# Spectral mixing weights loaded once and copied to four partition bands by TensorE, in a Fourier tokenizer with a transformer block

## The chip, the cores and the metric

The kernel runs on one core of one Trainium2 chip. The metric is the device time of one execution in microseconds (us), as the median of several runs. A core has a matrix engine (TensorE, PE in the profile, with its weight loads shown as PEld), a vector engine (VectorE, DVE), a scalar engine (ScalarE, ACT), a general engine (GpSimd, POOL) and a queue engine (SyncE, SP). Any of the last three may issue DMA transfers. SBUF is the on-chip memory of 128 partitions, PSUM the memory that TensorE writes to.

## The reference, cut to what matters

A batch of 64 images of 256 x 256 is lifted to C = 32 channels and passed through four Fourier layers. In each, the spectrum's lowest modes (12 rows from the top and 12 from the bottom, by 12 columns) are multiplied by complex weights that mix the channels. The result joins 77 text tokens and goes through one attention and one feed-forward layer.

```python
h = jnp.concatenate([x, gx, gy], axis=-1)
v = jnp.transpose(h @ p_w + p_b, (0, 3, 1, 2))          # 64 x 32 x 256 x 256
for i in range(4):
    W1 = fw1[i, ..., 0] + 1j * fw1[i, ..., 1]            # 32 in x 32 out x 12 x 12
    W2 = fw2[i, ..., 0] + 1j * fw2[i, ..., 1]
    x_ft = jnp.fft.rfft2(v)
    out_ft[:, :, :12, :12] = einsum('bixy,ioxy->boxy', x_ft[:, :, :12, :12], W1)
    out_ft[:, :, -12:, :12] = einsum('bixy,ioxy->boxy', x_ft[:, :, -12:, :12], W2)
    x1 = jnp.fft.irfft2(out_ft)
    x2 = einsum('bcxy,cd->bdxy', v, w_w[i]) + w_b[i]
    v = batchnorm(x1 + x2)                               # relu, but after the last
out = einsum('bcxy,cu->bxyu', v, q_w) + q_b              # 64 x 256 x 256
h = concatenate([out, txt], axis=1)                      # 64 x 333 x 256
h = h + attention(layernorm(h))
h = h + ffn_on_the_top_half_of_tokens(layernorm(h))
```

The weights `fw1` and `fw2` of one layer are 1.18 MB each, in f32, with the input channel first.

## The kernel before

The program is a sequence of stages. `forward_first` (L215) transforms the input images into the first spectrum `xh`. Then, for each Fourier layer `i`, `mix` (L410) multiplies the spectrum by the weights and writes the result to DRAM (`mix_d`). Between two mixes `layer` (L526) goes through all 64 images: it transforms back, adds the 1 x 1 product, applies the normalisation and the relu, and transforms the new values forward, storing a piece of the next spectrum for each image (`xh<-xo`, L783). After the fourth mix the constants of the transformer are loaded (from L843), the first image rows are read (`am`, L944; `hp`, L964) and the transformer runs.

*How a mix is tiled.* The 12 columns of modes are cut in 3 groups `g` of 4. The four columns of a group stand on four bands of 32 partitions, with the 32 input channels of a column in each band. So `xh` and the weight tiles `wm0`, `wm1` (one for each of `fw1`, `fw2`) have 128 partitions. A row of `mix` (loop over `kp`, 12 of them) takes two rows of modes: 48 matmuls (L437) with one band of `xh` as the stationary operand and one band of `wm` as the moving one. ACT copies the PSUM result to `e` (L449). ACT and DVE build from it the two parts of the output block `ob` (L454 to L457) and the sums for the normalisation (L460 to L474). SP stores the block by two DMAs (L475). There are three `ob` buffers in turn, cleared once by POOL (L421). After the loop the DVE chain and the square root (L482 to L510) give the scale and shift of the layer.

*How the weights come in.* `mix_weights` (L375) gives a function `piece(m)` for eight pieces: two weight tensors by four blocks of 8 output channels. A piece is a tile `wn` of 128 partitions, into which the same block is loaded four times, once for each band (L387), each time shifted by one column so that an index of column 0 in band `k4` is the weight of column `k4`:

```python
wn[C * k4:C * k4 + C, 0:n - 2 * k4],
fw[i, :, 8 * oh:8 * oh + 8].rearrange("c o k l r -> c (o k l r)")[:, 2 * k4:],
```

Then four copies bring the real and imaginary parts into the slots of `wm`: ACT into slots 0 (negated, L402) and 1 (L404), DVE into slots 3 and 4 (L406). Slot 5 is cleared (L392) and slot 2 filled with the 1 x 1 weights (L393) by POOL, with the first piece of each tensor. All the copies read `wn` with a stride of 1152 bytes between neighbouring output channels.

*Order.* For `i` = 0 the loads go on SP's queue, two pieces after the image loop of `forward_first`, and two after each of the three groups of its last transform; `wn` has two buffers. For the later layers the loads are on POOL's queue with four buffers: four pieces, then the load of the first 56 images of the spectrum (`xh` early, L826), the last 8 on SP (`xh` late, L829), `squares` (L513, which ends with the copy of `u2`, L523), and four more pieces. The buffers of `wn`, `xh` and `wm` lie over those of the layer before, so that a load waits for its last reader there. Elsewhere the order is written out, but the mixing weights and the constants stand in the order that a scheduler gives. In the program before, the ACT queue issues most of the transformer's constants (L854 to L899) among the rows of the fourth mix.

Of the kernel before, what the change touches and what calls it, by code (L numbers as in the profile page):

```python
# [17 lines left out]
C = 32  # L18
M = 12
# [134 lines left out]
def tile_fno_fusion_transformer(ctx: ExitStack, tc: tile.TileContext, a, cst_d, grid_d, out):  # L154
# [57 lines left out]
    w4 = [w4all[:, i, :] for i in range(L)]  # L212
    w0row = const.tile([128, 4, C], F32, name="w0row")

    def forward_first(xh, weights):  # L215


        u2 = const.tile([128, C], F32, name="u2_0")
# [1 line left out]
        with tc.tile_pool(name="f0", bufs=1) as fp, tc.tile_pool(name="f0i", bufs=3) as ip, \  # L220
# [41 lines left out]
                        accum_out=sq[:, b0 // 2 + n:b0 // 2 + n + 1],  # L262
                    )

            weights(0)
            weights(1)

            pw, pb = a["L0_tok_p_w"], a["L0_tok_p_b"].rearrange("(o c) -> o c", o=1)
            pwR = fp.tile([128, C], F32, name="pwR")
# [45 lines left out]
                    n += 1  # L315
            nc.scalar.copy(xm, ps[:, 0, :kn * B])

            for kyg in range(3):
                for ri in range(2):
                    t2 = [pq.tile([128, 2, 512], F32, name="xps") for _ in range(2)]  # L320
                    for j in range(4):
                        nc.tensor.matmul(
                            t2[j // 2][:, j % 2, :kn * B],
                            lhsT=px[32 * j:32 * j + KX, kyg, ri].rearrange("p q c -> p (q c)"),
                            rhs=xm[32 * j:32 * j + KX], start=True, stop=True, skip_group_check=True,
                        )
                    for j in range(2):
                        k0 = 2 * kn * j
                        nc.vector.tensor_tensor(
                            xh[:, kyg, ri, k0:k0 + 2 * kn, :].rearrange("p (j k) b -> p j k b", j=2),  # L330
                            t2[j][:, :, :kn * B].rearrange("p j (k b) -> p j k b", b=B),
                            g[:, kyg, ri, k0:k0 + 2 * kn, :].rearrange("p (j k) o -> p j k o", j=2)
                            .to_broadcast([128, 2, kn, B]),
                            ALU.add,
                        )
                weights(2 * kyg + 2)
                weights(2 * kyg + 3)


            mo = fp.tile([128, 4], F32, name="mo")  # L340
# [34 lines left out]
    def mix_weights(i, wmp, wnp):  # L375

        wms = [wmp.tile([128, 3, M, 6, C], F32, name=f"wm{half}") for half in range(2)]

        def piece(m):
            half, oh = divmod(m, 4)
            wm, fw = wms[half], a[f"L0_tok_fw{half + 1}"]
            n = 8 * M * M * 2
            wn = wnp.tile([128, n], F32, name="wn")
            for k4 in range(4):
                (nc.gpsimd if i else nc.sync).dma_start(  # L387
                    wn[C * k4:C * k4 + C, 0:n - 2 * k4],
                    fw[i, :, 8 * oh:8 * oh + 8].rearrange("c o k l r -> c (o k l r)")[:, 2 * k4:],
                )  # L390
            if oh == 0:
                nc.gpsimd.memset(wm[:, :, :, 5, :], 0.0)  # L392
                nc.gpsimd.tensor_copy(  # L393
                    wm[:, :, :, 2, :].rearrange("p g k o -> p (g k) o"),
                    w4[i].rearrange("p (o c) -> p o c", o=1).to_broadcast([128, 3 * M, C]),
                )
            v = wn.rearrange("p (o k g q r) -> p g k o q r", o=8, k=M, g=3, q=4)
            for slot, ri in ((4, 1), (3, 0), (1, 0), (0, 1)):
                s_ = v[:, :, :, :, 0, ri]
                d_ = wm[:, :, :, slot, 8 * oh:8 * oh + 8]  # L400
                if slot == 0:
                    nc.scalar.mul(d_, s_, -1.0)  # L402
                elif slot == 1:
                    nc.scalar.copy(d_, s_)  # L404
                else:
                    nc.vector.tensor_copy(d_, s_)  # L406

        return wms, piece

    def mix(i, lhs, wm, u2):  # L410


        halves = [slice(0, 128)] if B == 64 else [slice(0, B), slice(64, 64 + B)]
# [2 lines left out]
        with tc.tile_pool(name="mo", bufs=1) as op, tc.tile_pool(name="me", bufs=3) as ep, \  # L416
# [8 lines left out]
            nc.vector.memset(fr, 0.0)  # L425
            fin = op.tile([128, 2, C], F32, name="fin")
            nc.vector.memset(fin, 0.0)
            for kp in range(M):
                ps = pp.tile([128, 4, 512], F32, name="mps")
                wk, k0 = wm[2 * kp // M], 2 * kp % M  # L430
                for g in range(3):
                    for ri in range(2):
                        w0 = 32 * ri
                        for kk in range(2):
                            for k4 in range(4):
                                band = slice(C * k4, C * k4 + C)
                                nc.tensor.matmul(  # L437
                                    ps[64 * kk:64 * kk + B, k4, 128 * g + w0:128 * g + 128],
                                    lhsT=lhs(band, g, ri, 2 * kp + kk),
                                    rhs=wk[band, g, k0 + kk, 2 - 2 * ri:6 - 3 * ri, :].rearrange("p s o -> p (s o)"),  # L440
                                    start=ri == 0, stop=ri == 1, skip_group_check=True,
                                )
                e = ep.tile([128, 3, 4, 4, C], F32, name="e")
                a_ = ep.tile([128, 12, 2, C], F32, name="a_")
                o0, o1 = (
                    ob[kp % NB][:, p, :, :KX].rearrange("p o (n k) -> p n k o", k=M) for p in range(2)
                )
                for hv in halves:
                    nc.scalar.copy(  # L449
                        e[hv].rearrange("p g q s o -> p q g (s o)"),  # L450
                        ps[hv, :, 0:384].rearrange("p q (g s) -> p q g s", g=3),
                    )
                    ev = e[hv].rearrange("p g q s o -> p (g q) s o")
                    nc.scalar.mul(o1[hv, 0], ev[:, :, 2, :], -1.0)  # L454
                    nc.scalar.copy(o1[hv, 1], ev[:, :, 1, :])
                    nc.vector.tensor_copy(o0[hv, 0], ev[:, :, 1, :])
                    nc.vector.tensor_copy(o0[hv, 1], ev[:, :, 2, :])  # L457
                    nc.vector.tensor_copy(f0[hv, kp], ev[:, 0, 1:3, :])
                    for n, (us, fs) in enumerate(((0, 1), (3, 2))):
                        nc.vector.scalar_tensor_tensor(  # L460
                            a_[hv, :, n, :], ev[:, :, us, :], 2.0, ev[:, :, fs, :], ALU.mult, ALU.add
                        )
                    if kp == 0:
                        nc.vector.tensor_mul(acc[hv], a_[hv], ev[:, :, 1:3, :])
                    else:
                        nc.vector.tensor_mul(a_[hv], a_[hv], ev[:, :, 1:3, :])
                        nc.vector.tensor_add(acc[hv], acc[hv], a_[hv])
                if kp == 0:
                    nc.vector.tensor_add(fin[0:B, 1, :], e[0:B, 0, 0, 1, :], e[0:B, 0, 0, 0, :])
                for kk in range(2):  # L470
                    to = (M - kp) % M if kk == 0 else M - 1 - kp
                    hv = slice(64 * kk, 64 * kk + B)
                    if kk or kp != M // 2:
                        nc.scalar.copy(fr[hv, to], e[hv, 0, 0, 1:3, :])  # L474
                    nc.sync.dma_start(  # L475
                        mix_d[i][:, :, 2 * kp + kk, :], ob[kp % NB][hv].rearrange("b p o k -> b p (o k)")
                    )
# [331 lines left out]
    st = None  # L809
    acc = None  # L810
    for i in range(L):
        with tc.tile_pool(name="wn", bufs=4 if i else 2, reuse_waits="tile") as wnp, \
                tc.tile_pool(name="xh", bufs=1, reuse_waits="tile") as xp, \
                tc.tile_pool(name="wm", bufs=1, reuse_waits="tile") as wmp:
            wm, piece = mix_weights(i, wmp, wnp)
            if i == 0:
                xh = xp.tile([128, 3, 2, KX, B], F32, name="xh")
                u2 = forward_first(xh, piece)
                lhs = lambda band, g, ri, k: xh[band, g, ri, k, :]
            else:  # L820
                xh = xp.tile([128, B, 3, 2, KX], F32, name="xh")
                early = max(B - 8, 0)
                for m in range(4):
                    piece(m)
                if early:
                    nc.gpsimd.dma_start(  # L826
                        xh[:, :early].rearrange("p b g r k -> p b (g r k)"), xh_d[i - 1][:, :early]
                    )
                nc.sync.dma_start(  # L829
                    xh[:, early:].rearrange("p b g r k -> p b (g r k)"), xh_d[i - 1][:, early:]  # L830
                )
# [384 lines left out]
```

## Time and profile before

| what | value |
|---|---|
| time, median of 3 runs | 11381.7 us (11377.09 to 11388.17) |
| the profiled execution: its own time, its span | 11393.82 us, 11392.0 us |
| mean granted TensorE clock | 0.975 |
| busy: PE, DVE, ACT, POOL | 10594.2, 8460.5, 6496.0, 1477.9 us |
| first mix, from the first loads of weights to the last row | about 60 to 170 us |
| second, third and fourth mix, from `u2` to the end of the rows | 2554 to 2645, 5586 to 5685, 8633 to 8747 us |
| start of the transformer: load of the first `am` | 8763.1 us |

The profile is of one execution, and its times are microseconds from the start of the span. A line of the timeline gives the start, the length, the engine, the line of the kernel, the operation with output and input tile, and how many were merged ("x32"). In square brackets stands the idle time of the engine before it and what ended that. An engine with a "q" (SPq, ACTq, POOLq) is the queue that issues DMAs. A line of the waits gives who waited for whom: total time, number of waits, and the longest. The clock is a share of full speed, and the DMA share is how busy the 16 DMA engines of the core were.

### The profile page before, as it was taken

To read this page: it belongs to the slowest core of one execution; us is meant where nothing else is said; L and a number is where in the kernel's file an instruction comes from. 1 tells how busy PE (TensorE), PEld (TensorE's weight loads), DVE (VectorE), ACT (ScalarE), POOL (GpSimd) and SP (SyncE) were. 2 spreads that over 40 slices of the span, in tenths; PEclk is the share of its full clock that TensorE was granted. 3 is DMA by queue.
4 is the path that set the end of the run, shared out by engine and by line. 5 is a ranking of instruction groups with operands and counts; after the bars stand their busy time and mean duration, and the time that the engine had idled before them with its cause. 6 is when DMAs were issued, how large, how long until landed. Compare 5 with 4: busy or idle time off the path is not lost. (4 is left out here: it accounts for less than half of the span.)

```text
span 11392.0 us, 408517 instructions
## 1 busy us (share of the span) xinstructions
PE 10594.2 (93%) x182038; PEld 5729.6 (50%) x182038; DVE 8460.5 (74%) x10405; ACT 6496.0 (57%) x10697; POOL 1477.9 (13%) x2243
## 2 busy tenths in 40 slices
PE   6999999997999999999699999999995999999998
PEld 3555555543444444444344444444443666666666
DVE  5888888886777777777677777777775666666665
ACT  5777777775656655665556566565653333333333
POOL 0111111110000000000100000000001333333333
PEclk7999999998999999999899999999997999999999
DMA  7776676769999999999899999999998555555553
GB/s 233 248 248 244 247 250 246 248 238 326 378 383 376 383 379 375 376 380 380 296 374 383 379 383 380 377 373 371 382 376 279 224 222 224 228 230 227 229 227 135
DMA packets 977151, 3485.52 MB, mean 306 GB/s; under 512 B 151320, under 2 KB 200856, under 8 KB 905368
## 3 DMA queue, kind: packets, MB, share of 16 engines
q1 hardware_dynamic: 906880, 3376.23, 77.5%
q0 software_dynamic: 61360, 79.44, 3.1%
q8 instruction: 1424, 23.33, 0.8%
q10 hardware_dynamic: 7144, 3.72, 0.1%
q14 instruction: 343, 2.81, 0.1%
HBM read 1761.87 MB, written 1696.92 MB: 304 GB/s over the span
## 5 line engine op out<-in xcount | busy, mean ns | idle before, releaser
L721 ACT ACTIVATE ring<-ring 128x1024 f32<-128x1024 f32 x3072 | 3115.8, 1014 | 1182.0 <-PE ring L710 1116.4
L699 DVE STREAM_TRANSPOSE t<-vo 128x2048 f32<-128x2048 f32 x1536 | 3465.1, 2286 | 20.5 <-DVE vo L687 0.5
L710 PE MATMUL ring<-vo,w 32*32 32x512 f32 x49152 | 2411.8, 600 | 85.8 <-ACT vo L685 71.0
L687 DVE TENSOR_SCALAR vo<-ring 128x1024 f32<-128x1024 f32 x1280 | 1544.7, 1221 | 1195.4 <-PE ring L673 806.4
L685 ACT ACTIVATE vo<-ring 128x1024 f32<-128x1024 f32 x1792 | 1792.0, 1023 | 1043.3 <-PE ring L673 494.5
L732 PE MATMUL ring<-t,cst 32*32 32x512 f32 x49152 | 2072.6, 599 | 47.1 <-issue 40.8
L732 PEld LDWEIGHTS ring<-t,cst 32*32 32x32 f32 x49152 | 911.6, 103 | 924.9 <-issue 617.6
L710 PEld LDWEIGHTS ring<-vo,w 32*32 32x32 f32 x49152 | 802.2, 103 | 1071.6 <-issue 398.9
L611 POOL TENSOR_TENSOR ams<-ams,bns 48x512 f32<-48x512 f32 x384 | 401.4, 1045 | 6980.6 <-DMA ams<-mix 6710.2
L662 PE MATMUL ring<-cst,y 24*128 24x256 f32 x16384 | 1228.0, 402 | 76.2 <-DVE vo L687 58.2
L673 PE MATMUL ring<-vin,ws 32*32 32x512 f32 x32768 | 1281.2, 602 | 18.6 <-issue 13.2
L662 PEld LDWEIGHTS ring<-cst,y 24*128 24x128 f32 x16384 | 787.6, 185 | 989.7 <-DVE vo L687 389.0
L650 DVE STREAM_TRANSPOSE y<-ring 128x1024 f32<-128x1024 f32 x384 | 762.9, 1987 | 327.1 <-PE ring L642 326.2
L662 PE MATMUL ring<-mv,y 29*128 29x256 f32 x8192 | 703.8, 404 | 36.6 <-ACT ring L721 19.7
L662 PEld LDWEIGHTS ring<-mv,y 29*128 29x128 f32 x8192 | 455.2, 185 | 368.8 <-ACT ring L721 211.3
L766 PEld LDWEIGHTS ring<-cst,zt 128*128 128x128 f32 x4608 | 533.2, 193 | 178.3 <-ACT vo L685 114.3
L742 ACT COPY half<-ring 128x1024 f32<-128x1024 f32 x192 | 194.4, 1013 | 727.2 <-PE ring L732 727.1
L1165 POOL DMA_DIRECT2D out_dram<-o x1024 | 510.9, 507 | 660.6 <-DVE o L1160 617.6
L721 ACT ACTIVATION_READ_ACCUMULATOR ring<-ring 128x1 f32 x3072 | 584.9, 190 | 0.0
L766 PE MATMUL ring<-cst,zt 128*128 128x96 f32 x4608 | 565.3, 279 | 7.9 <-DVE zt L750 7.3
L750 DVE STREAM_TRANSPOSE zt<-ring 128x1024 f32<-128x1024 f32 x192 | 377.0, 1963 | 244.6 <-PE ring L732 244.6
L642 PE MATMUL ring<-ams,cst 49*128 49x512 f32 (+1 forms) x1536 | 450.3, 642 | 104.9 <-POOL ams L611 38.4
(367 smaller groups left out, 9812.4 us busy)
## 6 DMA issues: line engine op xcount, KB each, us to landing
v<-vo SPq DMA_DIRECT2D x3072, 512.0 KB, 7.9
vin<-v SPq DMA_DIRECT2D x2048, 512.0 KB, 9.1
ch<-v SPq DMA_DIRECT2D x512, 1024.0 KB, 12.6
mix<-ob SPq DMA_DIRECT2D x96, 512.0 KB, 5.7
ams<-mix SPq DMA_DIRECT2D x384, 96.0 KB, 8.0
xin<-in_x_dram SPq DMA_DIRECT2D x16, 1024.0 KB, 7.0
mv<-in_x_dram POOLq DMA_DIRECT2D x256, 64.0 KB, 7.5
out_dram<-o POOLq DMA_DIRECT2D x1024, 16.0 KB, 3.0
```

Source lines behind the costliest of these rows:

```text
L642: nc.tensor.matmul(ps[:, n, :], lhsT=EX[hv, 128 * h:128 * h + 128], rhs=ams[b % 2][hv], start=True, stop=True, skip_group_check=True,)
L650: nc.vector.transpose(y_[b, h].rearrange("p q c -> p c q"), ring[key][0][1].rearrange("p n (c k) -> p (n c) k", k=32),)
L662: nc.tensor.matmul(ps[n][:, 256 * r:256 * r + 256], lhsT=y_[b, t // 4][32 * n:32 * n + K, q:q + 4, :].rearrange("p q c -> p (q c)"), rhs=m ...
L673: nc.tensor.matmul(ps[n][32 * j:32 * j + 32], lhsT=ws[32 * n:32 * n + 32], rhs=v[32 * n:32 * n + 32, 2 * j:2 * j + 2, :], start=False, sto ...
L685: nc.scalar.activation(to, ring[key][h][1], AF.Relu)
L687: nc.vector.tensor_scalar(to, ring[key][h][1], 0.0, None, ALU.max)
L699: nc.vector.transpose(t32[b, t // 2][:, :, 8 * (t % 2):8 * (t % 2) + 8, :].rearrange("p y s c -> p s y c"), vo[b, t].rearrange("p s (y l) ...
L710: nc.tensor.matmul(ps[n][32 * j:32 * j + 32], lhsT=w4[i + 1][32 * n:32 * n + 32], rhs=vo[b, t][32 * n:32 * n + 32, 2 * j:2 * j + 2, :], st ...
L721: nc.scalar.activation(ps, ps, AF.Square, accum_out=acc[:, at:at + 1])
L732: nc.tensor.matmul(ps[n][32 * j:32 * j + 32], lhsT=FYT[32 * n:32 * n + 32, k, :], rhs=t32[b, j][32 * n:32 * n + 32, k].rearrange("p s c -> ...
L766: nc.tensor.matmul(ps[:, 0, 96 * g:96 * g + 96], lhsT=zt_[:, h, k0:k0 + 4, :].rearrange("p k c -> p (k c)"), rhs=FX[:, h, 48 * r:48 * r + ...
L1165: nc.gpsimd.dma_start(out[b, 64 * n + 16 * g:64 * n + 16 * g + 16].rearrange("(p t) d -> p t d", t=2), o[32 * g + 8 * n:32 * g + 8 * n + 8 ...
```

## The change

Each weight block is loaded once. There are now two tiles `wn0`, `wn1` of 128 partitions, one for each weight tensor, whose four bands hold the four blocks of 8 output channels. `load` issues the eight DMAs, on POOL for every layer. `fill` does the clearing and filling of slots 5 and 2. `spread` brings one or two blocks to the four bands: for each part (real, imaginary) and each band a matmul with a 32 x 32 identity block as stationary operand, and with the band's columns of the block as moving operand, puts 288 elements into that band of a PSUM tile. From there the same ACT and DVE copies go into `wm`. In the first mix eight spreads of one block run in `forward_first`, ahead of the last transform (PSUM tiles `xps`, three buffers). In the later mixes four spreads of two blocks run at the start of `mix` (PSUM tiles `mps`, two buffers).

```diff
-        def piece(m):
-            half, oh = divmod(m, 4)
-            wm, fw = wms[half], a[f"L0_tok_fw{half + 1}"]
-            n = 8 * M * M * 2
-            wn = wnp.tile([128, n], F32, name="wn")
-            for k4 in range(4):
-                (nc.gpsimd if i else nc.sync).dma_start(
-                    wn[C * k4:C * k4 + C, 0:n - 2 * k4],
-                    fw[i, :, 8 * oh:8 * oh + 8].rearrange("c o k l r -> c (o k l r)")[:, 2 * k4:],
-                )
-            if oh == 0:
+        wns = [wnp.tile([128, n], F32, name=f"wn{half}") for half in range(2)]
+        def load():
+            for half in range(2):
+                fw = a[f"L0_tok_fw{half + 1}"]
+                for oh in range(4):
+                    nc.gpsimd.dma_start(
+                        wns[half][C * oh:C * oh + C],
+                        fw[i, :, 8 * oh:8 * oh + 8].rearrange("c o k l r -> c (o k l r)"),
+                    )
+        def fill():
+            for wm in wms:
                 nc.gpsimd.memset(wm[:, :, :, 5, :], 0.0)
                 nc.gpsimd.tensor_copy(
...
-            v = wn.rearrange("p (o k g q r) -> p g k o q r", o=8, k=M, g=3, q=4)
+        def spread(m, count, ps):
+            half, oh = divmod(m, 4)
+            v = wns[half].rearrange("p (o k g q r) -> p g k o q r", o=8, k=M, g=3, q=4)
+            for j in range(count):
+                row = slice(C * (oh + j), C * (oh + j) + C)
+                for ri in range(2):
+                    for k4 in range(4):
+                        nc.tensor.matmul(
+                            ps[C * k4:C * k4 + C, 2 * j + ri, 0:24 * M].rearrange("p (g k o) -> p g k o", g=3, k=M),
+                            lhsT=ID[row, row], rhs=v[row, :, :, :, k4, ri], start=True, stop=True,
+                            skip_group_check=True, tile_position=(C * (oh + j), C * k4),
+                        )
             for slot, ri in ((4, 1), (3, 0), (1, 0), (0, 1)):
-                s_ = v[:, :, :, :, 0, ri]
-                d_ = wm[:, :, :, slot, 8 * oh:8 * oh + 8]
+                s_ = ps[:, :, 0:24 * M].rearrange("p (j r) (g o) -> p r g j o", r=2, o=8)[:, ri]
+                d_ = wms[half][:, :, :, slot, 8 * oh:8 * (oh + count)].rearrange(
+                    "p g k (j o) -> p (g k) j o", o=8
+                )
...
# forward_first
-            weights(0)
-            weights(1)
+            load()
+            fill()
...
+            for m in range(8):
+                spread(m, 1, pq.tile([128, 2, 512], F32, name="xps"))
             for kyg in range(3):
...
-                weights(2 * kyg + 2)
-                weights(2 * kyg + 3)
...
# mix
+            for m in range(0, 8 if spread else 0, 2):
+                spread(m, 2, pp.tile([128, 4, 512], F32, name="mps"))
             for kp in range(M):
...
# main loop
-        with tc.tile_pool(name="wn", bufs=4 if i else 2, reuse_waits="tile") as wnp, \
+        with tc.tile_pool(name="wn", bufs=1, reuse_waits="tile") as wnp, \
...
-                for m in range(4):
-                    piece(m)
+                load()
...
-                for m in range(4, 8):
-                    piece(m)
+                fill()
                 lhs = lambda band, g, ri, k: xh[band, :, g, ri, k]
             with tc.manual_schedule():
-                st = mix(i, lhs, wm, u2)
+                st = mix(i, lhs, wm, u2, spread if i else None)
```

In the order in which the scheduler now sets the instructions, the loads of the first mix are the first on POOL's queue, at the start of the program. In the fourth mix four of the transformer's constants are issued by ACT ahead of the last row's last copy, nine more ahead of the square root, and the rest after it.

More of the change, by code (lines that the diff above doesn't have):

```diff
@@ L213, in tile_fno_fusion_transformer, with forward_first @@
     w0row = const.tile([128, 4, C], F32, name="w0row")
-    def forward_first(xh, weights):
+    def forward_first(xh, load, fill, spread):
         u2 = const.tile([128, C], F32, name="u2_0")
@@ L375, in mix_weights @@
     def mix_weights(i, wmp, wnp):
+        n = 8 * M * M * 2
         wms = [wmp.tile([128, 3, M, 6, C], F32, name=f"wm{half}") for half in range(2)]
-        def piece(m):
-            half, oh = divmod(m, 4)
-            wm, fw = wms[half], a[f"L0_tok_fw{half + 1}"]
-            n = 8 * M * M * 2
-            wn = wnp.tile([128, n], F32, name="wn")
-            for k4 in range(4):
-                (nc.gpsimd if i else nc.sync).dma_start(
-                    wn[C * k4:C * k4 + C, 0:n - 2 * k4],
-                    fw[i, :, 8 * oh:8 * oh + 8].rearrange("c o k l r -> c (o k l r)")[:, 2 * k4:],
-                )
-            if oh == 0:
+        wns = [wnp.tile([128, n], F32, name=f"wn{half}") for half in range(2)]
[9 more added lines that the diff above has]
+            for wm in wms:
                 nc.gpsimd.memset(wm[:, :, :, 5, :], 0.0)
@@ L406, in piece, with mix @@
                     nc.vector.tensor_copy(d_, s_)
-        return wms, piece
-    def mix(i, lhs, wm, u2):
+        return wms, load, fill, spread
+    def mix(i, lhs, wm, u2, spread):
         halves = [slice(0, 128)] if B == 64 else [slice(0, B), slice(64, 64 + B)]
@@ L811, in tile_fno_fusion_transformer @@
     for i in range(L):
-        with tc.tile_pool(name="wn", bufs=4 if i else 2, reuse_waits="tile") as wnp, \
+        with tc.tile_pool(name="wn", bufs=1, reuse_waits="tile") as wnp, \
                 tc.tile_pool(name="xh", bufs=1, reuse_waits="tile") as xp, \
                 tc.tile_pool(name="wm", bufs=1, reuse_waits="tile") as wmp:
-            wm, piece = mix_weights(i, wmp, wnp)
+            wm, load, fill, spread = mix_weights(i, wmp, wnp)
             if i == 0:
                 xh = xp.tile([128, 3, 2, KX, B], F32, name="xh")
-                u2 = forward_first(xh, piece)
+                u2 = forward_first(xh, load, fill, spread)
                 lhs = lambda band, g, ri, k: xh[band, g, ri, k, :]
```

## The prediction

> **What bounds the kernel now.** The page's busy table first: 10.6 of 11.4 ms on TensorE (PE), but those are the layers and the transformer, which the diff leaves alone. It touches the four mixing stages, too short for the page's forty slices. So I read the timeline and the waits around the second mix (2546 to 2602 us).
>
> ```profile
> 2554.25 0.19 DVE L523 COPY u<-ps 128x32 f32<-128x32 f32 x1 [3.19 <-PE ps L522]
> ...
> 2576.75 3.69 PE L437 MATMUL mps<-wm,xh 32*64 32x128 f32 x136 [22.53 <-DMA xh<-xh]
> ...
> 2598.96 0.71 ACT L404 COPY wm<-wn 128x288 f32<-128x288 f32 x1 [2.47 <-DMA wn<-in_L_tok_fw_dram]
> ...
> 2601.37 1.44 ACT L449 COPY e<-mps 128x1536 f32<-128x1536 f32 x1
> ```
>
> From the end of the layer (L523) to the second row's copy `e` (kp=1) 47.1 us pass in which PE does some 8 us of mixing. First the spectrum `xh` is late, then the weights. The waits view of the same window gives the sums:
>
> ```profile
> DVE wm L406 <- DMA wn<-in_L_tok_fw_dram: 34.4, 6, 14.0
> PE mps L437 <- DMA xh<-xh: 22.5, 1, 22.5
> ACT wm L404 <- DMA wn<-in_L_tok_fw_dram: 21.2, 6, 5.4
> ```
>
> The by-engine windows (busy PE, PEld, DVE, ACT, POOL, then TensorE clock, DMA share, GB/s) tell the loading part from the steady rows, where ACT paces a row at 3.4 to 3.5 us with DMA at 0.97:
>
> ```profile
> 2546.00:2602.00 56.00, 12.61 (x316) 11.21 (x314) 18.05 (x29) 15.71 (x24) 20.37 (x29) 0.58 0.74 199
> 2602.00:2645.00 43.00, 22.17 (x864) 19.43 (x864) 41.94 (x80) 36.48 (x54) 0.00 (x0) 0.62 0.97 281
> ```
>
> The third and fourth mix wait longer, 55.3 us from L523 (5586.14) to the kp=1 copy (5641.60), and 55.2 (8632.77 to 8688.18). In the first mix the 32 weight loads stand on SP's queue ahead of the first stores of `ob`:
>
> ```profile
> 59.63 68.75 SPq L387 DMA_DIRECT2D wn<-in_L_tok_fw_dram  x32
> 128.48 40.47 SPq L475 DMA_DIRECT2D mix<-ob  x24
> 138.71 1.44 ACT L449 COPY e<-mps 128x1536 f32<-128x1536 f32 x1
> ```
>
> With three `ob` buffers the fourth row (kp=3) cannot go on before 136.8; from kp=4's copy at 138.71 the rows run at the pace of the stores.
>
> **What the Trainium skill says.** "TensorE: Matmul & The Clock Gate", Part 3 (row/col tiling): tiles at distinct positions run concurrently, but a weight load overlaps running matmuls only where the row group differs. The spreads keep one row group and change the column group. This trace has a relative, L310 (four column groups, all rows): 32 instructions of 384 columns take 2.79 us, 87 ns apart, though one lasts 486. So column groups do overlap here. Part 1 of that page (the clock gate): idle halves the clock; the trace agrees, at 0.50 between 2562 and 2576 us. "SBUF — State Buffer", Specifications: lines of 16 B, at least two hits each for full speed. The spreads read their moving operand at a stride of 1152 B. The trace shows strided reads cost: 668 ns for 288 elements at L406, where a contiguous copy from PSUM takes 0.29 us for 128 and 0.69 for 512. "DMA: Bandwidth & Descriptors", Issuing engines are not separate DMA queues: transfers of SP and POOL share 16 engines. So fewer bytes help `xh` too.
>
> **Part by part.**
>
> *Loads.* Per mix 32 DMAs of 287 to 288 KB (9.4 MB) become 8 of 288 KB (2.4 MB), 24 issues of 492 ns less on POOL (SP in the first mix). They now have buffers of their own (`wn0`, `wn1`), so none waits for copies out of an older piece. From the second mix on, they and `xh` early are issued as the layer's last tiles leave their addresses, about 2493, 2528 and 2537 us, and no longer behind the memset of `wm` that waits for the last stored spectrum. At the 361 GB/s shown for 2562 to 2576, `xh` early (4.0 MB) needs 11 us; with the layer's stores beside it 19 as before. It lands by 2556 instead of 2579. `xh` late lands 3.6 us after 2555.2. All of it lies beside the spreads: zero, covered by them.
>
> *Spreads.* Per mix 8 blocks × 2 parts × 4 bands = 64 f32 matmuls of 288 columns, which are 128 instructions (the 48 calls of a row at L437 show as x96). No row shows this shape, so two bounds. Below: L310's 87 ns for 384 columns at full clock, times 288/384, 65 ns. Above: no overlap at all; one instruction of 512 columns lasts 600 ns in the layers (L710), so 288 at half clock 600 × 288/512 × 2 = 675. Between them, at the clock of this place: a row of L437 is 96 instructions of 112 columns on average in 2.57 us, 27 ns each with eight tiles (four row groups by two column halves); 288 columns on four tiles are 27 × 288/112 × 2 = 139. I take **140 ns**, 17.9 us per mix. The third pair of blocks waits for the copies of the first (two PSUM buffers); behind it on PE stand the later pairs and kp=0, so PE is the queue where a slow copy would show.
>
> *Copies out of PSUM.* DVE and ACT copied 16 pieces each of 288 elements (668 and 709 ns). Now, from the second mix on, 8 each of 576 out of PSUM: from 0.29/0.69 us (DVE, 128/512) and 0.37/1.44 (ACT, 256/1536) I get 0.76 and 0.64. ACT's follow DVE's, 2.8 us per pair of blocks. Behind them on ACT and DVE only kp=0's work is queued, which needs them anyway. They hide behind the next pair's 4.5 us, save the last.
>
> *Second mix.* Spreads can start when `u2` is out, 2554.4: done 2572.4, last copies 2575.2; kp=0's matmuls (2.6 us) beside them; its `e` copy 2575.2; kp=1's one row (3.4) later, 2578.6 against 2601.37: **-22.8**. *Third, fourth:* the same 24.2 us from `u2` to kp=1 against 55.3: **-31.1 each**.
>
> *First mix.* The loads go to POOL at the start, beside `xin`: 2.3 MB at the start displace the first `xin`, about +2 us on a loop that first waits for it. `xm` is out at 75.3. The clock is full to about 80, so some 77 instructions at 65 ns, then 51 at 140: +12.1 us before the `xh` chain, less 2.4 of DVE copies that stood in it. `u2` ends near 105 instead of 94.7, the `ob` memset behind it; kp=0's `e` near 108, kp=4's at 108 + 4×3.45 = 121.8, and no load stands in front of the stores: 138.71 - 121.8 - 2 = **-15**.
>
> *The transformer's constants.* In the fourth mix their ACT issues (L854 to L899, some 20 us of ACT in all) now stand among kp=1 to 11: 54.4 us where the second mix takes 38.4. The new order puts them behind the loop: -16 there, and the chain from the last constant (`won`) to the first image row then ends about 16 later: **0** for both together.
>
> *Sum.* -22.8 - 31.1 - 31.1 - 15 = **-100** on the profiled 11393.8 us (span 11392.0, 0.1% above the median 11381.7): about **11282** on the median.
>
> **The rivals.** About 0.2% (23 us) is what a measurement of this kernel tells from no change.
>
> (a) *The spreads pace lower than I take.* The stride costs nothing, or PE warms up: 60 ns. Then copies bound, some 11 us per mix, and the sum is -126: 11256. For it: L710's and L732's sixteen tiles issue at 37 ns. Against it: the clock is 0.50 at the very place.
>
> (b) *The spreads turn into the wait.* They share a row group and each loads an identity block first; if that does not overlap, or the strided moving operand comes at the pace of one line per element, an instruction takes 300 to 675 ns. The gain of the second mix is gone at (17.9+22.8)/128 = 0.32 us, that of the third at 0.38, of the first at about 0.25. So slower than before from some 0.33 us on; at 550 ns it is (0.55-0.14)×128×4 = +210 on -100: +110, 11490. At 300 ns: (0.30-0.14)×128×4 = +82 on -100, -18: no change. For it: the page's row group sentence and the 2.1 ns per element of L406. Against it: L310.
>
> (c) *The constants cost the start of the transformer more than they gave.* `am` waits for a load that ACT issues late; if a constant of 1 MB lands late too, +16 to +25: 11298 to 11307. For it: ACT issues everything in order. Against it: DMA is free there.
>
> (d) *The loads go, but `xh` stays the wait.* PE waited 22.5 us for `xh` alone. If `xh` early still cannot start before the last stored spectrum (2555.2), it lands 11 to 19 us later, 2566 to 2574, and kp=0 behind the spreads (2572.4) starts on time or 2 us late; if the layer's last stores hold it longer, at 2580 to 2590, each later mix gains 8 to 18 us less: 11306 to 11336. For it: one DMA of 4 MB on 16 shared engines. Against it: its buffer comes free at 2537.
>
> **How the numbers follow.** My case 0.52, (a) 0.13, (c) 0.12, (d) 0.10, (b) 0.13, of it 0.04 near no change and 0.09 slower. The range reaches from 11240, which is (a) with the constants' 16 us kept in the loop's favour, to 11350, a little over (d) with part of (c); it leaves out (b). Faster is the sum of the others, 0.87; same 0.04, slower 0.09.
>
> **What would show it.** In the profile after: eight load issues per mix on POOL; the new matmuls as x128 at 140 ns each, about 18 us from `u2`; PE's wait for `xh` gone; the kp=1 copy 24 us after `u2`; the first mix's stores of `ob` no longer behind 68.75 us of loads; the constants after the twelfth row, and `am` about 36 us after the last `e`. Wrong if the spreads' spacing is above 0.3 us, if rows wait for `xh`, or if the transformer's first `hp` comes later than the fourth mix's gain.

## The result, and the profile after

The changed kernel takes 11280.44 us (median of 4 runs, 11276.35 to 11293.58), the one before 11383.88 us beside it. The medians are 103 us apart. The ratio is 0.9912, with a 95% interval from 0.9899 to 0.9924, some 100 us less. The prediction was 11282. The table cuts the two profiled executions (spans 11392.0 and 11291.7 us) at the points that the prediction used. "u2" is the copy that ends the layer, "kp" a row's copy to `e`; all are taken from start to start.

| stretch, us | before | after | difference | predicted |
|---|---|---|---|---|
| start to kp=4 of the first mix | 138.71 | 134.06 | -4.7 | -15 |
| kp=4 to kp=11 of the first mix | 23.88 | 23.91 | 0.0 | 0 |
| first layer, to u2 | 2391.66 | 2387.30 | -4.4 | 0 |
| second mix, u2 to kp=1 | 47.12 | 17.33 | -29.8 | -22.8 |
| its rows, then the second layer | 2984.77 | 3000.15 | +15.4 | 0 |
| third mix, u2 to kp=1 | 55.46 | 20.89 | -34.6 | -31.1 |
| its rows, then the third layer | 2991.17 | 2991.80 | +0.6 | 0 |
| fourth mix, u2 to kp=1 | 55.41 | 22.80 | -32.6 | -31.1 |
| its rows, kp=1 to kp=11 | 52.96 | 36.20 | -16.8 | -16 |
| kp=11 to the first `am` | 22.00 | 36.16 | +14.2 | +16 |
| first `am` to the end | 2628.86 | 2621.10 | -7.8 | 0 |

The differences add to -100.3. The second layer's +15 and the last stretch's -8 are put down to scatter. Over the 14 profiled executions of all kernels of this study the second layer took 2943 to 2963 us and the last stretch 2618 to 2630, whatever had been changed. The first layer too varied, from 2381 to 2392, in all but one of them (below). The stretch from u2 to kp=1 scatters less: over the four kernels of this study whose three later mixes are the same, it took 16.7 to 17.3, 20.3 to 23.8 and 21.0 to 23.1 us.

The timeline of the second mix after the change, in the form that the prediction showed (L543 is the copy of `u2`, L409 the spreads, L469 the copy to `e`):

```profile
2545.27 0.19 DVE L543 COPY u<-ps 128x32 f32<-128x32 f32 x1 [4.36 <-PE ps L542]
...
2545.52 4.60 PE L409 MATMUL mps<-wn,cst 32*32 32x288 f32 x64 [0.28 <-DVE u L543]
...
2551.11 4.57 PE L409 MATMUL mps<-wn,cst 32*32 32x288 f32 x64 [1.00 <-ACT wm L420]
...
2556.34 3.31 PE L457 MATMUL mps<-wm,xh 32*64 32x128 f32 x128 [0.66 <-issue]
...
2562.60 1.44 ACT L469 COPY e<-mps 128x1536 f32<-128x1536 f32 x1
```

Nothing here waits for a weight or for `xh`. PE goes from `u2` into the spreads, 64 matmuls of two instructions each, 128 instructions in 9.2 us, and then into the rows. (Below, a time per spread is that of one instruction.) The waits view of 2545 to 2562 us has no DMA left among its large entries, but for PE's 0.4 us ahead of the last product of the layer:

```profile
ACT wm L422 <- DVE wm L424: 9.1, 4, 5.3
DVE wm L424 <- PE mps L409: 5.1, 4, 2.0
...
PE ps L542 <- DMA xh<-xh: 0.4, 1, 0.4
```

The start of the program is another matter. First the timeline, then SP's waits:

```profile
1.29 4.04 POOL L388 DMA_DIRECT2D wn<-in_L_tok_fw_dram  x8 [0.84 <-POOLq L1216]
...
22.69 50.03 SPq L235 DMA_DIRECT2D xin<-in_x_dram  x16
...
29.79 1.12 PE L239 MATMUL ups<-xin,cst 128*64 128x512 f32 x2 [29.79 <-DMA xin<-in_x_dram]
```

```profile
SPq L235 <- DMA w<-in_L_tok_w_w_dram: 14.6, 1, 14.6
```

The first image load is issued at 22.69 us where it was at 7.71, and the first image matmul starts 13.9 us later than before. SP stood 14.6 us on a wait for the loads of `w4` (L211, four of 16 KB), which ran beside the 2.4 MB of weights. The DMA view shows what held them, for each queue the packets, the MB and the share of the 16 engines' time between 8 and 20 us (q0 is POOL's queue; q10, by its loads, ACT's):

```profile
q0 software_dynamic: 308, 1.92, 72.6%
q10 hardware_dynamic: 315, 0.06, 4.1%
```

The small packets of ACT's queue came through at 315 in 12 us. Between 20 and 23 us, as the last packets of the weights pass, 646 came through. In the kernel before, 838 did between 6 and 8 us.

### The profile page after: what moved, and what is told of

Same layout as the page of the kernel before. It is cut to its first block, busy times and chain, and to the rows that moved or that the text cites. A ratio compares the mean times of both kernels' runs of the same rounds, so it can differ in the third digit from the quotient of the medians.

```text
span 11291.7 us, 409300 instructions
## 1 busy us (share of the span) xinstructions
PE 10625.0 (94%) x182550; PEld 5738.0 (51%) x182550; DVE 8446.5 (75%) x10381; ACT 6473.1 (57%) x10673; POOL 1442.4 (13%) x2179
## 4 chain that ended last, share of the span: by engine, by line
PE 62%; DMA 20%; DVE 9%; ACT 3%; issue 3%; SPq 2%; POOL 0%; ACTq 0%; DVEq 0%; POOLq 0%
PE ring L752 15%; DMA v<-vo 11%; PE ring L682 9%; PE ring L730 8%; DMA vin<-v 6%; PE ring L693 5%; PE hp L982 4%; PE ring L662 3%; PE pp L1145 3%; PE pp L1156 3%; PE ring L786 2%; DVE vo L707 2%; PE pp L1110 2%; PE pp L1175 2%; PE pp L1072 1%
## 5 line engine op out<-in xcount | busy, mean ns | idle before, releaser
L693 PE MATMUL ring<-vin,ws 32*32 32x512 f32 x32768 | 1287.8, 603 | 22.9 <-issue 16.2
## 6 DMA issues: line engine op xcount, KB each, us to landing
ch<-v SPq DMA_DIRECT2D x512, 1024.0 KB, 12.5
```

Source lines behind the costliest of these rows:

```text
L693: nc.tensor.matmul(ps[n][32 * j:32 * j + 32], lhsT=ws[32 * n:32 * n + 32], rhs=v[32 * n:32 * n + 32, 2 * j:2 * j + 2, :], start=False, sto ...
```

## The experiments

The edits of some 10 us below cannot be told apart from the changed kernel by whole times: their 95% intervals overlap with its 0.9899 to 0.9924. They are read from the stretches of their profiles, one for each kernel, against the scatter given above.

### The first mix: loads behind the images, or the whole first mix as before

```diff
-                    nc.gpsimd.dma_start(
+                    (nc.gpsimd if i else nc.sync).dma_start(
                         wns[half][C * oh:C * oh + C],
```

> The eight weight loads of the first mix are issued by SP behind the sixteen loads of the image loop, and no longer by POOL at the start; nothing else differs from the changed kernel. Theory A (at the start the weight loads hold up the small load of w4, and with it the wait that stands ahead of the first image load on SP): the first image matmul comes at about 16 us again and not at 29.8, every later point of the first mix 13 us earlier, the time about 11267. Rival (the first mix is set by its stores or by the rest of its chain, the late start is hidden): the first image matmul moves, the end of the first mix moves by less than 3 us, time 11280.

Measured: 11269.41 us, ratio 0.9898 (0.9884 to 0.9913) to the kernel before. The first image matmul starts at 16.26, kp=4 comes at 120.63 where it was 134.06, and kp=11 13.1 us earlier. Theory A holds: the chain to the first mix's end has next to no slack for a late start. The profile confirms the cause: SP issues all images before the weights, and its waits for `w4` are 0.8 us in all:

```profile
7.70 51.66 SPq L235 DMA_DIRECT2D xin<-in_x_dram  x16
59.41 5.93 SPq L388 DMA_DIRECT2D wn<-in_L_tok_fw_dram  x8
```

The second run keeps the later mixes of the changed kernel and goes back in the first:

```diff
 # forward_first
-            load()
-            fill()
+            weights(0)
+            weights(1)
...
-            for m in range(8):
-                spread(m, 1, pq.tile([128, 2, 512], F32, name="xps"))
...
+                weights(2 * kyg + 2)
+                weights(2 * kyg + 3)
```

> The first mix is the one of the kernel before (32 loads on SP, no spreads there); the other three are those of the changed kernel. Theory A (the first mix gave only 5 us at its end and 4 in the layer behind it, the three others all the rest): 8 to 10 us slower than the changed kernel, about 11289. Rival (each mix gave a quarter of the gain): 25 us slower, about 11306.

Measured: 11291.75 us, ratio 0.9915 (0.9898 to 0.9931). The first mix ends at 162.55 (changed kernel 157.97), 4.6 us later, and the layer behind it takes 2386.4, as in the changed kernel. So the first mix gave 4 to 5 us, as Theory A has it, and the 4.4 us in the first layer were not its doing. The Rival's 25 us are not there: the three later mixes gave the rest.

### What of the old wait was bytes, what was the queue

In the kernel before, only the spectrum's place on POOL's queue is changed:

```diff
+                if early:
+                    nc.gpsimd.dma_start(xh[:, :early]..., xh_d[i - 1][:, :early])
                 for m in range(4):
                     piece(m)
-                if early:
...
```

> The kernel before with one edit: on POOL's queue the load of the first 56 images of the spectrum stands ahead of the first four pieces of weights, and no longer behind them and the clearing of wm. Loads, bytes and buffers stay those of the kernel before. Theory A (the spectrum was late because of its place in the queue, but the 9.4 MB of weight loads then end last: at some 370 GB/s they and the spectrum need 36 us from about 2537): PE's wait for xh shrinks, the kp=1 copy comes 40 to 43 us after u2 in the three later mixes where it came 47 and 55; 15 to 30 us faster than before in all, so not the 98 us of the change. Rival (the place in the queue was all of it, the repeated loads cost nothing): kp=1 about 25 to 30 us after u2, 60 to 90 us faster than before.

Measured: ratio 0.9994 (0.9985 to 1.0002), no change; kp=1 comes 48.9, 55.0 and 55.5 us after u2. Both expectations fail. The waits of 2545 to 2610 us tell why:

```profile
PE mps L437 <- DVE wm L406: 26.0, 1, 26.0
...
POOL wm L392 <- DMA xh<-xo: 20.4, 1, 20.4
POOL wn L387 <- DMA wn<-in_L_tok_fw_dram: 10.2, 12, 1.8
```

PE's wait changed its name and kept its length: 22.5 us for `xh` became 26.0 us for `wm`. POOL still stops 20.4 us at the clearing of `wm`, which waits for the last stored spectrum, and most of the weight loads stand behind it. Weights and spectrum were late to about the same extent, so bringing one forward gains nothing. The edit was not quite clean: in the second mix the first weight loads now stand behind the spectrum's in the queue and go at 2527.54, where four went at 2493.79.

The other side, the 32 loads in buffers that no copy has to clear first, was tried in two ways.

```diff
                     nc.gpsimd.dma_start(wns[half]...)
+                    for rep in range(3 if i else 0):
+                        nc.gpsimd.dma_start(again[3 * (4 * half + oh) + rep], fw[i, ...])
```

> In the second to fourth mix each block is read three times more, into scratch memory in DRAM that nothing reads, on POOL's queue behind the block's own load: the number of loads and bytes read of the kernel before, with the buffers of the changed one. Theory A (the four times larger loads, which the spectrum's load stands behind, made xh late in the kernel before): xh comes 12 to 20 us later, the kp=1 copy 10 to 20 us later in each of the three mixes, the time about 11325. Rival (the wait for free wn buffers and for the memset that stood ahead of xh was all of it; bytes are free): within 8 us of the changed kernel, 11280 to 11288.

Measured: 11321.85 us, but this says nothing on the question. Nothing held the extra loads to their place, and all 72, of all three mixes, were issued between 25.7 and 300.2 us, beside the first mix. It then ended at 188.48 us where it was 157.97, and the first layer took 2404.8. What it shows is that some 20 MB of other loads there cost 30 us in that mix.

```diff
-            for half in range(2):
+            for half in [0, 1] * (4 if i else 1):
```

> In the second to fourth mix the eight loads of the changed kernel are issued four times over, into the same places and with the same data: 32 loads and 9.4 MB as in the kernel before, but in buffers that no copy has to clear, and all of them ahead of the spectrum's load on POOL. Theory A (bytes cost little; waits for buffers and the memset in the queue made most of the wait before): 24 more loads at some 1.2 us each end about 10 to 20 us later than in the changed kernel, so kp=1 comes 7 to 12 us later after u2 in each of the three mixes, 24 to 35 us after it and not 47 to 55; about +30, 11310. Rival 1 (the bytes were the whole of it): kp=1 at 40 us or more after u2, 11340 or more. Rival 2 (bytes are free): kp=1 as in the changed kernel, 11280.

Measured: 11331.97 us, ratio 0.9955 (0.9939 to 0.9972). kp=1 comes 34.2, 39.5 and 42.2 us after u2: 16.8, 18.6 and 19.4 us later than in the changed kernel, 54.8 in all. That lies between Theory A (7 to 12 each) and Rival 1 (40 us and more after u2).

```profile
2551.03 0.49 POOL L388 DMA_DIRECT2D wn<-in_L_tok_fw_dram  x1 [0.60 <-DMA wn<-in_L_tok_fw_dram]
...
2552.37 5.82 PE L409 MATMUL mps<-wn,cst 32*32 32x288 f32 x64 [8.01 <-DMA wn<-in_L_tok_fw_dram]
...
2552.87 0.56 POOL L845 DMA_DIRECT2D xh<-xh  x1 [1.34 <-DMA xh<-xo]
...
2572.35 3.31 PE L457 MATMUL mps<-wm,xh 32*64 32x128 f32 x128 [8.74 <-DMA xh<-xh]
```

The last of the 32 is issued at 2551.03 and the spectrum at 2552.87 where the changed kernel issues it at 2532.84. PE waits 8.0 us for the weights and then 8.7 us for the spectrum. In the three mixes the change took 97.0 us from the stretch between u2 and kp=1 (29.8 + 34.6 + 32.6). Issuing the blocks four times puts 54.8 of them back. That is not the price of the bytes alone: the run has a wait of its own, because a load into a place that is still being loaded waits for the one before it (POOL's 0.60 on `wn` in the first line above). The other 42 are what this run did not restore: the four buffers, the clearing of `wm` in the queue's way, and the copies out of strided SBUF, less the spreads, which the kernel before did not have. These were not told apart.

### What a spread costs

```diff
-                for ri in range(2):
+                for ri in (0, 0, 1, 1):
```

> Every spread matmul is issued twice (the second overwrites the first with the same values), so 128 instructions more in each mix. Theory A (the spreads are on the path wherever nothing else is late): 9.2 us more in the first and in the second mix, 4 to 6 in the third and 2 to 5 in the fourth, where the copies wait for the last spectrum's store while the spreads run; about +25, 11305. Rival 1 (the spreads hide behind the spectrum's load or the store): +0 to 9, only the first mix. Rival 2 (the second half is slower than the first because the array or its clock fills up): more than +37.

Measured: 11312.94 us, ratio 0.9937 (0.9923 to 0.9952). kp=0 of the first mix comes 8.3 us later than in the changed kernel; u2 to kp=1 grows by 9.4, 9.2 and 6.3. Theory A holds, with even less cover in the third and fourth mix than it expected; nothing grows by clearly more than the 9.2 us that 128 take.

The next three ask what sets that price. Each ran once (11272.06, 11278.37 and 11279.52 us), and only its pace is read. The price does not follow the clock. The windows of the changed kernel (length, PE busy, clock, DMA share, GB/s) hold 64 instructions each:

```profile
2545.52:2550.12 4.60, 4.60 (x64) 0.55 0.25 52
5563.00:5567.60 4.60, 4.60 (x64) 0.56 0.84 357
8575.69:8580.24 4.55, 4.55 (x64) 1.00 0.97 414
```

71 to 72 ns from one to the next, at a clock of 0.55 as at 1.00.

```diff
-    rhs=v[row, :, :, :, k4, ri]
+    rhs=wns[half][row, 576 * k4 + 288 * ri:576 * k4 + 288 * ri + 288]
```

> The moving operand of each spread is 288 neighbouring elements of the block, and not 288 with strides of 1152 and 96 bytes, so that the weights land in another order in wm; shapes, counts, buffers and waits are those of the changed kernel. Theory B (the strided read sets the 71.5 ns between spreads, since it is the same at a clock of 1.00 and of 0.50): the spacing falls, to 60 ns or less at full clock and changes with the clock. Rival (issue on one row group sets it): 71 to 72 ns as before.

This kernel leaves out the right order of the weights and serves for the pace alone. The windows of that run, with 48 instructions in the first and 64 in the others (the count takes in neighbours):

```profile
87.20:89.10 1.90, 1.89 (x52) 1.00 0.00 0
2537.10:2541.40 4.30, 4.30 (x64) 0.50 0.24 44
8549.80:8552.20 2.40, 2.39 (x64) 1.00 1.01 430
```

From neighbouring elements 64 take 4.38 us at half clock (68 ns each) and 2.44 at full clock (38 ns). So the strided read is a floor of 71.5 ns, which hardly shows at half clock and nearly doubles the price at full clock. Theory B is right. It agrees with what "SBUF — State Buffer", Specifications, in the Trainium skill says: its 16-byte lines want at least two hits each for full bandwidth, and the strided read takes one element of a line. The prediction cited this, but its 140 ns have no term for the stride.

```diff
-            for j in range(count):
-                row = slice(C * (oh + j), C * (oh + j) + C)
-                for ri in range(2):
-                    for k4 in range(4):
+            for ri in range(2):
+                for k4 in range(4):
+                    for j in range(count):
+                        row = slice(C * (oh + j), C * (oh + j) + C)
```

> In the spreads of two blocks (second to fourth mix) the two blocks, which lie in different row groups, take turns from matmul to matmul; in the changed kernel all of one block come first. Theory B (each tile's own read of a strided operand sets the pace; 4 tiles were busy, now 8): the spacing falls from 71.5 to 36 to 50 ns, a pair of blocks from 2.3 to 1.2 to 1.6 us. Rival (the order does not matter; the issue of one matmul every 71 ns does): 71 to 72 ns.

Measured: 64 of two row groups in turn take 3.57 us, 56 ns each, in all three later mixes.

```profile
5550.84 3.57 PE L409 MATMUL mps<-wn,cst 32*32 32x288 f32 x64 [0.28 <-DVE u L543]
```

That is between the two expectations. The floor belongs at least in part to what one row group reads, but eight tiles do not bring half of it. u2 to kp=1 is 1.0 to 1.4 us shorter, which hardly stands out of the scatter.

```diff
-                for ri in range(2):
-                    for k4 in range(4):
+                for k4 in range(4):
+                    for ri in range(2):
```

> The real and the imaginary part of a band follow each other, so four instructions in a row use one tile position and then the next; in the changed kernel two do. This is the case that the prediction's rival on the spreads needs. Theory A (what makes the spreads cheap is that neighbouring column groups overlap): the spacing rises, to between 90 and 290 ns, and the mixes lose up to 28 us each. Rival (position does not matter): 71 to 72 ns.

Measured: 4.65 to 4.70 us for 64, 73 ns each.

```profile
5553.54 4.70 PE L409 MATMUL mps<-wn,cst 32*32 32x288 f32 x64 [0.28 <-DVE u L543]
```

My theory fails and the rival holds: with four instructions in a row on one position the pace is the same. So it is not needed that neighbours in the stream change the column group. This does not rule out that the four column groups overlap, if several instructions can wait at each; a run with all spreads on one column group would tell, and was not made. By the records, whose ends are modelled, one instruction lasts 687 ns, so nearly ten are under way at a time. What lets them follow so closely stays open. "TensorE: Matmul & The Clock Gate", Part 3, has weight loads overlap running matmuls only where the row group differs. In the second mix of the changed kernel the 128 loads (PEld at L409) take 131 ns each, 16.8 us in all, within 9.2 us in which PE is never without a matmul, and the 16 instructions of a block keep one row group. So the measurement decides against a rule that strict. The same part also names a background weight buffer; whether that is at work here no run shows.

### The new wait behind the spreads

In the third and fourth mix PE waits between the two pairs of spreads. The fourth, in the changed kernel:

```profile
8574.97 0.32 SPq L803 DMA_DIRECT2D xh<-xo  x1
8584.32 0.32 SPq L848 DMA_DIRECT2D xh<-xh  x1
...
8584.62 2.75 DVE L424 COPY wm<-mps 128x576 f32<-128x576 f32 x4 [8.11 <-DMA xh<-xo]
...
8587.52 4.60 PE L409 MATMUL mps<-wn,cst 32*32 32x288 f32 x64 [7.28 <-ACT wm L420]
```

The first copies into `wm` wait until the last 72 KB of the spectrum are stored. `wm0` lies over the buffers of `xo`. And that store takes 9.4 us beside the 4 MB load of the spectrum, issued at 8569.73. In the kernel before, where that load came only after it, SP could go on 1.9 us after the same store:

```profile
8632.07 0.32 SPq L783 DMA_DIRECT2D xh<-xo  x1
8633.99 0.32 SPq L829 DMA_DIRECT2D xh<-xh  x1
```

```diff
-            op, yp, cp, xp, zp, tp = (
+            op, yp, cp, zp, tp, xp = (
                 pool(n, k, reuse_waits="tile")
-                for n, k in (("lo", 4), ("ly", 1), ("lc", 1), ("lx", 2), ("lz", 1), ("lt", 6))
+                for n, k in (("lo", 4), ("ly", 1), ("lc", 1), ("lz", 1), ("lt", 6), ("lx", 2))
```

> In the layers the buffers of the spectrum pieces (xo) are allocated behind those of the turned images, so that the mixing weights of the next mix no longer lie over them; nothing else differs from the changed kernel. Theory A (the copies into wm wait for the last store of xo, which runs beside the 4 MB load of the spectrum; PE waits 1.0, 4.5 and 7.3 us for them in the three later mixes): those waits go, the rows begin when the last 8 images of the spectrum have landed, the kp=1 copy comes 1 to 5 us earlier after u2 in each; about -9 in all, 11271. Rival (the last images' load, which waits for the same store, ends last anyway): the copies move, the kp=1 copy moves by less than 1 us, time 11280.

Measured: 11270.86 us, ratio 0.9898 (0.9884 to 0.9913). u2 to kp=1 is 16.5, 17.2 and 16.4 us: 0.8, 3.7 and 6.4 less than in the changed kernel. Theory A holds; in the third and fourth mix the gain is well outside the scatter. In the fourth the two pairs of spreads now follow each other:

```profile
8553.01 4.57 PE L409 MATMUL mps<-wn,cst 32*32 32x288 f32 x64 [0.28 <-DVE u L543]
8558.41 4.59 PE L409 MATMUL mps<-wn,cst 32*32 32x288 f32 x64 [0.83 <-ACT wm L420]
```

### The transformer's constants

```diff
-    nc.scalar.dma_start(hbias, ...)      # and the 17 other constants
+    nc.gpsimd.dma_start(hbias, ...)
```

> The transformer's 18 constant loads are issued by POOL, which has nothing to do there, and no longer by ACT; all else as in the changed kernel. Theory A (the first image row waits for the last constant, which ACT issues late behind the fourth mix's work): the first load of am comes 22 to 28 us after the last e copy and not 36, about -11, 11269. Rival (the constants wait for the buffers of the last row in any case): 34 to 36 us and 11280.

Measured: 11287.40 us, ratio 0.9916 (0.9901 to 0.9931); from kp=11 to the first `am` 37.1 us, as before the edit. The rival holds.

```profile
8622.91 0.54 POOL L872 DMA_DIRECT2D hbias<-in_L_tok_q_b_dram  x1 [42.77 <-PE mps L457]
...
8638.78 0.72 POOL L917 DMA_DIRECT2D won<-in_L_attn_Wo_dram  x1
...
8650.24 1.09 PE L922 MATMUL wtp<-cst,won 128*128 128x128 f32 x4 [12.30 <-issue]
```

The first of them cannot be issued before the last row's matmuls have released the buffers. The 18 then take 16 us to issue, waits between them included, and the last is used 11.5 us later. Moving the issue from ACT to POOL did not matter.

### Four edits together

> Four edits on the changed kernel together: the first mix's loads on SP behind the image loop, the xo buffers above the turned images, the constants on POOL, and the two blocks of a spread in turns. Theory A: the gains add, -13, -9, -11 and -3: about 11245. Rival (the third is given back where the transformer's first image rows and the constants share the DMA engines): 11256 or more.

The diffs are those shown above. Measured: 11262.95 us (11246.15 to 11273.17), ratio 0.9897 (0.988 to 0.9913), an interval that still overlaps with that of the changed kernel. The kernel before ran at 11392.25 us beside it: the medians are 129 us apart, and the ratio says 117 (99 to 137). In its trace the first mix ends at 145.16 (changed kernel 157.97), and u2 to kp=1 takes 16.2, 16.8 and 18.2 us. So the gains of the first two edits are there, 12.8 + 9.8 us. The turns add nothing that shows (the `xo` edit alone gave 10.9), and kp=11 to `am` is 35.8, no gain. Theory A's sum fails: two of its four terms are missing. The time is the Rival's, but not for its reason, since the constants' edit had no gain to give back. The profiled span, 11244.3 us, is the shortest of the study, though by whole times this kernel is not told apart from the first-mix or the `xo` edit alone.

## Why the prediction was right, and where it was not

*The mechanism held.* The weights' and the spectrum's waits went, and the spreads took their place on PE. The loads are all covered but in the first mix. The total of 11282 was within 2 us, but this is largely luck: the first mix gave 10.3 us less than forecast and the three others 7.0, 3.5 and 1.5 more.

*The price of a spread* was mis-sized: the step "27 × 288/112 × 2 = 139", rounded to 140 ns. It measured 71.5. Scaling L437's 27 ns by columns and tiles took for granted that its pace is set by columns. A contiguous spread at half clock takes 68, and worked back from that L437 would have 68 × 112/288 / 2 = 13 ns (an estimate): something else sets its 27, and no run shows what. The 17.9 us per mix were 9.2, 8.7 less. In the second mix 7.0 of them show (-29.8 for -22.8).

*A wait was missed.* The prediction let copies run from `u2` on. They wait for the last store of `xo`, which got slower because the spectrum's load, now early, runs beside it. PE waits 4.5 and 7.3 us in the third and fourth mix. With the 8.7 us above, that makes -35.3 and -32.5 of the forecast's -31.1; -34.6 and -32.6 were measured. So these came near the forecast by two errors of opposite sign. This is the cost of a transfer that starts sooner: not that it is late, but what it meets.

*The first mix's "+2 us on a loop that first waits for it"* was wrong: 13.9. The prediction gives no working for the 2, only the bytes that displace the first image. What stood ahead of the first image on SP was a wait for the four small loads of `w4`, on ACT's queue, and their packets were slow beside the weights'. -15 became -4.7. The rest of that term held: with the late start taken away (first_sp) kp=4 comes at 120.63, where "121.8" was worked out for a start without any delay. That the rows then "run at the pace of the stores" was misread: kp=4 to kp=11 took 3.41 us a row before, the pace that the same text gives for ACT, and 3.42 after.

*The constants'* -16 and +16 measured -16.8 and +14.2.

*The rivals.* (a), cheap spreads, came nearer on the price, 60 ns for 71.5, than the 140 that I took, but neither of its reasons is borne out. The clock was low in the second and third mix (0.55 and 0.56), and where it was full, in the fourth, the price was the same; and the stride does cost. Its -126 did not come: the late start (13.9) and the waits for the store (1.0 + 4.5 + 7.3) took about the difference back. So the total came out near 11282 by a price too high and two waits that were left out or put too low. (b), the spreads as the wait, would have needed 0.33 us. (Its "about 0.25" for the first mix is 0.21 by the prediction's own terms, (12.1 + 15)/128.) (c) and (d) did not come: `xh` is issued at 2532.84, before the last store, and lands in 12.5 to 14.2 us in the three mixes. The "2579" for its landing before was too late; PE starts on it at 2576.75.

## What to carry to other kernels

When two inputs of a stage are both late, taking one forward only changes the name of the wait; look for what both stand behind. A load that is moved to an idle queue at the start of a program need not be free: follow the small transfers that gate the first large one, and put it behind them. When a transfer starts earlier, list what runs in that time and who waits for it, down to the buffers that lie over each other.

## What the runs showed that I had not expected

The spacing of these f32 spreads from a strided operand was 71 to 72 ns at a clock of 0.55 and of 1.00; from a contiguous one 68 and 38 ns. Two row groups in turn gave 56 ns at a clock of 0.50, and with the four edits together 3.53 us for 64, 55 ns, at 1.00. Four instructions in a row on one tile position gave 73 ns. Four loads of 16 KB beside 2.4 MB of weight loads came some 14 us late, while ACT's queue moved 315 packets in 12 us.
